# Four image blocks with a selective scan on one Trainium2 core: operands of silu, rows of C and a normalisation move between engines

## Chip, cores, metric

The kernel runs on one core of one Trainium2 chip. The metric is the device time of one execution in microseconds (us). A core has five instruction streams that run beside each other and meet at semaphores: PE (TensorE, matrix products, with its weight loads shown as PEld), DVE (VectorE), ACT (ScalarE), POOL (GpSimd) and SP (SyncE, which here issues DMAs). Each takes its instructions in the order in which they were built.

## What is computed

The input is x, 4 images of 128 channels and 64 x 64 pixels (4096 columns), all in float32. Four layers follow, each adding to x what it makes of the group-normalised x (32 groups): attention over the 4096 pixels, a 5 x 5 convolution whose weights are built from tables, a selective scan, and a 3 x 3 convolution. The change lies mostly in the third:

```python
t = einsum('oc,bchw->bohw', Wx, x) + bx          # 128 channels; halves F and R
# one half, u of 64 channels; R runs over the flipped sequence
xc = silu(sum(conv_w[:, k] * up[:, k:k + L] for k in range(4)) + conv_b)
delta = softplus(xc.T @ Wd + bd);  Bm = xc.T @ WB;  Cm = xc.T @ WC
h = scan over the sequence of  h = exp(delta * A) * h + (delta * xc) * Bm   # 64 states a channel
y = sum over states of h * Cm  +  D * xc
```

## The kernel before

**Stages.** For each image b: attention (`attention_start`, `attention`), the 5 x 5 convolution (`conv_pairs`), then the preparation of the scan (`scan_prep`, `scan_operands`), and at last the scan itself (`scan_core`), 256 ticks an image. Afterwards `scan_end` and the 3 x 3 convolution (`conv`) finish an image. The scan of image b runs beside attention, convolution and preparation of image b + 1: `images` is a generator of all that work, and `program` pulls steps from it between the half-ticks of `scan_core`, by a credit of 2.8 a tick (1.5 for the last image) against the cost that each step yields. So the order on each engine is fixed when the program is built, and buffers and semaphores do the rest.

**One tick of the scan** covers 32 channels x 4 states on 1024 columns: `drive` multiplies on POOL (db, L1027), `decay` takes exp on ACT (da, L1020), `recur` scans on DVE (L1037), the product with C is on DVE (L1040) or on POOL (`weigh`, L1058) by `to_pool`, and `collect` sums on PE into y (L1072), every second tick.

**Preparation.** `scan_operands` cuts the 4096 columns into 8 blocks of 512 (i) and writes out an order by hand: a table of slots, five to a block, with each step at a slot. In image 0 nothing runs beside the first of it. For block i at slot t = 5 i:

- t, t + 1 `taps`: 4 taps x 2 halves = 8 products on PE (L832) into a bank "s", each half on its own 64 columns of the array; for i = 0 an edge term (L838)
- t + 4 `halves`: on ACT, half of the biased sum to xc (L846), and its tanh to th (L851): for image 0 a buffer in SBUF, for the others the bank itself
- t + 5 `silu`: on DVE, xc = (th + 1) * xc (L855)
- t + 8, t + 9, t + 12: the three products on PE with the block-diagonal weights `bdiag` (L864): 0 for delta, 1 for B, 2 for C. B and C share bank "a"
- t + 10 `softplus` (L877, L878), t + 12 `exp` (L904, L909) on ACT; t + 13 `digits` on DVE (L883, L884)
- t + 11 and t + 13 `row`: ACT copies a row block of B (m = 1) or C (m = 2) from PSUM to a buffer "w" (L869, four buffers), and SP writes it to DRAM

After a group of blocks come the logarithms on ACT (`logs`, L913), then `join` and `drives` on POOL (L889, L894).

**Next image.** Beside that, `start(b + 1)` loads the next x, and `attention_start` takes its statistics on DVE (L378), computes scale rs and offset nb on POOL (`group_norm`, L363, L364), normalises x in place in four pieces of 1024 columns on ACT (`piece`, L369 in `normalise`), and makes v: `keys` on PE (L396) and `take` on ACT (L401), for b > 0 in turns in one bank "s".

Of the kernel before, what the change touches and what calls it, by code (L numbers as in the profile page):

```python
# [24 lines left out]
F32 = mybir.dt.float32  # L25
I32 = mybir.dt.int32
AF = mybir.ActivationFunctionType
ALU = mybir.AluOpType
# [4 lines left out]
P = 128  # L33
# [3 lines left out]
MM = 512  # L37
HALF = P // 2
# [7 lines left out]
PRODUCT, HOP, SLOT, PACE, ENDPACE, AHEAD = 0.86, 1.7, 0.7, 2.8, 1.5, 4  # L46


BQ, BK, BX, BP, CONVB, BD, DSKIP, MAINB, CONVW, ALOG = 0, 1, 2, 3, 4, 5, 6, 7, 8, 12
# [3 lines left out]
def conv_preact_kernel(  # L53
# [16 lines left out]
    nc = tc.nc  # L70
# [12 lines left out]
    scale = float(C) ** -0.5  # L83
# [3 lines left out]
    const = ctx.enter_context(tc.tile_pool(name="const", bufs=1))  # L87
# [3 lines left out]
    pools, ready = {}, set()  # L91

    def bank(tag, name):
        return pools.get(tag, ps).tile([P, MM], F32, tag=tag, name=name)
# [20 lines left out]
    ident = const.tile([P, P], F32, name="ident")  # L115
    make_identity(nc, ident)
    ones = const.tile([P, P], F32, name="ones")
# [9 lines left out]
    def col(i):  # L127
        return vec[:, i : i + 1]


    ssm_sb = early.tile([P, 3, HALF], F32, name="ssm_sb")
    nc.scalar.dma_start(ssm_sb, ssm)
    bdiag = const.tile([P, 3, C], F32, name="bdiag")
    nc.gpsimd.memset(bdiag, 0.0)
    for d in range(2):
        r = slice(d * HALF, (d + 1) * HALF)
        nc.gpsimd.tensor_copy(bdiag[r, :, r], ssm_sb[r, :, :])


    NK, NQ = P // SG, NST // NI  # L140
# [10 lines left out]
    skip = const.tile([P, P], F32, name="skip")  # L151
# [25 lines left out]
    wtap = const.tile([P, KC, C], F32, name="wtap")  # L177
    edge = const.tile([P, KC - 1], F32, name="edge")
    cbias = small.tile([P, 1], F32, tag="cbias", bufs=1, name="cbias")
    hbias = const.tile([P, 1], F32, name="hbias")  # L180

    def scan_constants():

        for k in range(KC):
            ptap = bank("z", f"ptap{k}")[:, :C]
            nc.tensor.matmul(
                ptap, col(CONVW + k).to_broadcast([P, P]), ident, start=True, stop=True
            )
            yield HOP
            nc.vector.tensor_tensor(wtap[:, k, :], wm[:, 3, :], ptap, ALU.mult)  # L190
        for t in range(KC - 1):

            nc.vector.tensor_reduce(
                edge[:, t : t + 1], vec[:, CONVW : CONVW + KC - 1 - t], AX.X, ALU.add
            )
        nc.vector.tensor_tensor(cbias, edge[:, 0:1], col(CONVW + KC - 1), ALU.add)
        nc.vector.scalar_tensor_tensor(cbias, cbias, col(BX), col(CONVB), ALU.mult, ALU.add)
        nc.vector.tensor_scalar(edge, edge, col(BX), -1.0, ALU.mult, ALU.mult)
        nc.vector.tensor_scalar(hbias, cbias, 0.5, None, ALU.mult)
        yield HOP  # L200
        mine = early.tile([P, NI], F32, name="mine")
        nc.vector.tensor_reduce(
            mine, ident.rearrange("p (s i) -> p i s", i=NI), AX.X, ALU.add
        )
        rates = every.rearrange("p k q i -> p (k q) i")
        mine = mine.unsqueeze(1).to_broadcast([P, NK * NQ, NI])
        nc.vector.tensor_tensor(rates, rates, mine, ALU.mult)
        nc.vector.tensor_reduce(a_neg, rates, AX.X, ALU.add)
        yield HOP
        nc.scalar.activation(a_neg, a_neg, AF.Exp)  # L210
        nc.vector.tensor_reduce(
            sel, ident.rearrange("p (s i) -> p s i", i=NI), AX.X, ALU.add
        )
        nc.vector.tensor_scalar(skip, ident, col(DSKIP), None, ALU.mult)
        yield HOP
        nc.vector.tensor_scalar(a_neg, a_neg, -1.0, None, ALU.mult)
        yield HOP
# [66 lines left out]
    def large(n, name):  # L284
        return pools["big"].tile([P, ASIZE], F32, tag=f"A{n % 2}", name=name)
# [6 lines left out]
    def stats_tile(name):  # L292
        return small.tile([P, NM, 6], F32, tag=f"gn_st{name[0]}", name=f"st_{name}")
# [74 lines left out]
    def normalise(dst, src, gn):  # L368
        nc.scalar.activation(dst, src, AF.Identity, scale=gn[0], bias=gn[1])  # L369
# [4 lines left out]
    def attention_start(b, xn):  # L374

        st = stats_tile(f"a{b}")
        for i in range(NM):
            nc.vector.bn_stats(st[:, i, :], xn[:, bass.ts(i, MM)])  # L378
            yield 0.0
        gn = yield from group_norm(st, f"a{b}")  # L380
        while b > 0 and (b - 1, "taps") not in ready:
            yield 0.0
        v = pools["big"].tile([P, VSIZE], F32, tag="V", name=f"v_{b}")
        v = v[:, : NJT * C].rearrange("p (j c) -> p j c", c=C)
        pvs = {}

        def piece(i):
            cut = bass.ts(i, L // 4)
            normalise(xn[:, cut], xn[:, cut], gn)

        def keys(i):

            tag = "s" if b > 0 else "saz"[i % 3]
            pvs[i] = bank(tag, f"pv_{b}_{i}").rearrange("p (t c) -> p t c", c=C)
            for t in range(TPM):
                nc.tensor.matmul(  # L396
                    pvs[i][:, t, :], xn[:, bass.ts(i * TPM + t, P)], wv, start=True, stop=True
                )

        def take(i):  # L400
            nc.scalar.copy(v[:, i * TPM : (i + 1) * TPM, :], pvs.pop(i))  # L401

        piece(0)
        yield SLOT
        for i in range(NM):
            if i % 2 == 0 and i // 2 + 1 < 4:
                piece(i // 2 + 1)
            keys(i)
            yield SLOT
            if b > 0:  # L410
                take(i)
                yield 0.0
            elif i > 0:
                take(i - 1)
        if b == 0:
            take(NM - 1)
        return xn, v
# [394 lines left out]
    def scan_operands(b, xn, mats4, piece):  # L812
# [5 lines left out]
        xc = large(b, f"xc_{b}")[:, :L]  # L818
        delta = pools["big"].tile([P, L], F32, tag="xt", name=f"delta_{b}")
        pts, ths, pzs, pbs, us = {}, {}, {}, {}, {}  # L820

        def taps(i, *ks):
            if ks[0] == 0:
                pts[i] = bank("s", f"pt_{b}_{i}")
            pt = pts[i]
            t = i * MM
            for k in ks:
                lo = L + 2 * pad - 1 - k - t - (MM - 1)
                views = (xn[:, t + k : t + k + MM], xn[:, lo : lo + MM][:, ::-1])
                for d, view in enumerate(views):  # L830
                    r = slice(d * HALF, (d + 1) * HALF)
                    nc.tensor.matmul(  # L832
                        pt[r, :], wtap[:, k, r], view,
                        start=k == 0, stop=k == KC - 1,
                        tile_position=(0, d * HALF), skip_group_check=True,
                    )
                    if i == 0 and k == 0:
                        nc.tensor.matmul(  # L838
                            pt[r, : pad], ident[:, r], edge, start=False, stop=False,
                            tile_position=(0, d * HALF), skip_group_check=True,  # L840
                        )

        def halves(i):

            pt = pts.pop(i)
            nc.scalar.activation(xc[:, bass.ts(i, MM)], pt, AF.Identity, scale=0.5, bias=hbias)  # L846

            ths[i] = pt if b > 0 else pools["bg"].tile(
                [P, MM], F32, tag="w", bufs=4, name=f"th_{b}_{i}"
            )  # L850
            nc.scalar.activation(ths[i], pt, AF.Tanh, scale=0.5, bias=hbias)  # L851

        def silu(i):
            cut = bass.ts(i, MM)
            nc.vector.scalar_tensor_tensor(  # L855
                xc[:, cut], ths.pop(i), 1.0, xc[:, cut], ALU.add, ALU.mult
            )
            if i % 2:
                c = i // 2
                nc.sync.dma_start(xcd[c], xc[:, bass.ts(c, CH)])  # L860
# [5 lines left out]

        def row(i, m):
            bs = pools["bg"].tile([P, MM], F32, tag="w", bufs=4, name=f"bs{m}_{b}_{i}")
            nc.scalar.copy(bs, pbs.pop((i, m)))  # L869
            c, h = divmod(i, CH // MM)  # L870
            nc.sync.dma_start(bc[m - 1][c][:, bass.ts(h, MM)], bs)

# [271 lines left out]
    def program(safe):  # L1144
# [113 lines left out]
        with ExitStack() as es, tc.manual_schedule():  # L1258
# [18 lines left out]
            work = images()  # L1277
# [26 lines left out]
            def result():  # L1304

                while (B - 1, "staged") not in ready:
                    next(work)
                return ends[B - 1][2]

            credit = 0.0  # L1310
# [91 lines left out]
```

## Time and profile before

| what | value |
|---|---|
| time, median of 3 runs | 4535.0 us (4529.53 to 4537.47) |
| profiled execution: its time, its span | 4540.09 us, 4538.3 us |
| granted TensorE clock, mean | 0.939 |
| PE busy | 4022.5 us (89%) |
| DVE busy | 3649.1 us (80%) |
| POOL busy | 3636.2 us (80%) |
| ACT busy | 2400.1 us (53%) |
| bias and half, L846 ACT | 32 x 688 ns |
| tanh, L851 ACT | 24 x 660 ns to PSUM, 8 x 689 ns to SBUF |
| row copies, L869 ACT | 64 x 595 ns |
| normalisation of x, L369 ACT | 16 x 1245 ns |
| db, L1027 POOL | 1024 x 2366 ns |

Durations are those of single instructions; on ACT one starts up to 0.12 us before the one ahead of it ends, so that from start to start 128 x 512 takes 0.5 to 0.58 us. PE's ends are modelled: of its instructions the distance between starts is the safer number. An fp32 product stands as two records (passes). The page gives shares of the whole span; the views of the trace (windows, timelines, waits) give the same for any stretch. Where a wait has several causes, the view names the one that came last.

### The profile page before, as it was taken

What the parts mean: (1) busy time and instruction counts of PE and PEld (TensorE: products, weight loads), DVE (VectorE), ACT (ScalarE), POOL (GpSimd) and SP (SyncE); (2) the same over time, 40 slices, a digit from 0 to 9 for tenths busy, and PEclk for the clock granted to TensorE, in tenths of its full rate; (3) what the DMA queues carried; (4) which work ended last, traced back from release to release, by engine and by line L of the source; (5) the groups of instructions that cost most, each with busy time, mean ns of one, the idle gap of its engine ahead of it and who ended that gap; (6) DMA issues with size and microseconds to landing.
All of it is one profiled execution on the core that took longest, in us unless ns stands there. A gap on an engine that the chain in (4) does not pass through costs nothing. (4 is left out here: it accounts for less than half of the span.)

```text
span 4538.3 us, 43660 instructions
## 1 busy us (share of the span) xinstructions
PE 4022.5 (89%) x13568; PEld 1492.3 (33%) x13568; DVE 3649.1 (80%) x3619; ACT 2400.1 (53%) x4420; POOL 3636.2 (80%) x1730
## 2 busy tenths in 40 slices
PE   8999998999999979999999879999999658576767
PEld 4444433333333323333333223333333112121212
DVE  4722106999998978999989879999999699999993
ACT  3333217666665466666654566666654654544441
POOL 3433207999998969999989889999999799999992
PEclk9999999999999989999999989999999878687878
DMA  1000006445544555544545555545445566656561
GB/s 62 6 1 1 5 29 239 175 170 174 175 174 155 181 202 201 175 174 169 179 154 181 185 207 180 169 170 175 175 159 178 211 235 204 231 188 230 186 232 47
DMA packets 210579, 719.48 MB, mean 159 GB/s; under 512 B 24864, under 2 KB 25760, under 8 KB 210208
## 3 DMA queue, kind: packets, MB, share of 16 engines
q1 hardware_dynamic: 208736, 715.87, 44.8%
q8 instruction: 109, 1.79, 0.2%
q14 instruction: 134, 1.10, 0.1%
q10 hardware_dynamic: 1600, 0.73, 0.1%
HBM read 649.07 MB, written 67.44 MB: 158 GB/s over the span
## 5 line engine op out<-in xcount | busy, mean ns | idle before, releaser
L1027 POOL TENSOR_TENSOR db<-dx,br 128x1024 f32<-128x1024 f32 x1024 | 2399.7, 2366 | 234.0 <-DMA dx<-dxd 59.7
L1020 ACT ACTIVATE da<-de,a_neg 128x512 f32<-128x512 f32 (+1 forms) x1795 | 1342.2, 751 | 745.4 <-DVE da L1037 451.2
L464 PE MATMUL sc<-r,x 128*128 128x512 f32 x2048 | 1082.4, 611 | 18.2 <-ACT r L433 12.4
L476 PE MATMUL acc<-pt,v 128*128 128x512 f32 x2048 | 1046.6, 593 | 1.6
L1058 POOL TENSOR_TENSOR hc<-hc,cr 128x1024 f32<-128x1024 f32 x406 | 959.7, 2364 | 14.3 <-ACT last L1053 11.7
L470 ACT ACTIVATE pt<-sc 128x512 f32<-128x512 f32 x1024 | 604.3, 590 | 563.9 <-PE sc L464 555.2
L1072 PE MATMUL y<-hc,sel 128*32 128x512 f32 x4096 | 656.9, 651 | 271.5 <-POOL hc L1058 267.0
L1040 DVE TENSOR_TENSOR hc<-da,cr 128x512 f32<-128x512 f32 (+1 forms) x1067 | 828.4, 776 | 68.9 <-issue 1.8
L1037 DVE TENSOR_TENSOR_SCAN da<-da,last,db 128x512 f32<-128x512 f32 (+1 forms) x464 | 728.2, 1569 | 27.3 <-POOL db L1027 21.7
L1037 DVE TENSOR_TENSOR_SCAN da<-da,da,db 128x512 f32<-128x512 f32 x449 | 577.9, 1287 | 13.6 <-ACT da L1020 12.7
L464 PEld LDWEIGHTS sc<-r,x 128*128 128x128 f32 x2048 | 359.1, 190 | 605.0 <-issue 374.3
L476 PEld LDWEIGHTS acc<-pt,v 128*128 128x128 f32 x2048 | 387.5, 190 | 497.2 <-issue 477.9
L1037 DVE TENSOR_TENSOR_SCAN hc<-da,hc,db 128x512 f32<-128x512 f32 x322 | 413.1, 1283 | 61.2 <-ACT da L1020 30.4
L1037 DVE TENSOR_TENSOR_SCAN hc<-da,last,db 128x512 f32<-128x512 f32 (+1 forms) x304 | 455.9, 1500 | 6.6 <-ACT da L1020 2.4
L518 POOL TENSOR_TENSOR sidep<-sidep,pt 128x512 f32<-128x512 f32 x120 | 170.4, 1420 | 280.0 <-ACT pt L470 277.9
L1072 PEld LDWEIGHTS y<-hc,sel 128*32 128x32 f32 x4096 | 94.7, 111 | 728.5 <-POOL hc L1058 359.5
L643 PE MATMUL pcm<-xpm,cw 128*128 128x512 f32 x576 | 290.5, 652 | 30.5 <-ACT xpm L369 30.5
L760 PE MATMUL pe<-df,cw 128*128 128x512 f32 x640 | 289.5, 598 | 0.0
L518 DVE TENSOR_TENSOR sided<-sided,pt 128x512 f32<-128x512 f32 x120 | 97.2, 810 | 231.0 <-ACT pt L470 229.7
L1037 DVE TENSOR_TENSOR_SCAN da<-da,db 128x512 f32<-128x512 f32 (+1 forms) x154 | 231.2, 1501 | 32.5 <-POOL db L1027 16.4
L498 PE MATMUL zp<-pt,ones 128*32 128x512 f32 x1536 | 204.8, 595 | 5.0 <-DVE xs L562 5.0
L1053 ACT COPY last<-da 128x1 f32<-128x1 f32 x469 | 73.0, 156 | 246.9 <-DVE hc L1040 245.1
(196 smaller groups left out, 2719.5 us busy)
## 6 DMA issues: line engine op xcount, KB each, us to landing
br<-bm SPq DMA_DIRECT2D x512, 512.0 KB, 5.2
cr<-cm SPq DMA_DIRECT2D x512, 512.0 KB, 3.9
de<-dd SPq DMA_DIRECT2D x64, 512.0 KB, 4.6
dx<-dxd SPq DMA_DIRECT2D x64, 512.0 KB, 6.5
x<-in_x_dram SPq DMA_DIRECT2D x16, 512.0 KB, 5.1
xs<-in_x_dram SPq DMA_DIRECT2D x16, 512.0 KB, 5.6
xsd<-xs SPq DMA_DIRECT2D x16, 512.0 KB, 5.1
xcd<-xc SPq DMA_DIRECT2D x16, 512.0 KB, 2.8
```

What stands on the lines that cost most here:

```text
L464: nc.tensor.matmul(sc, xn[:, bass.ts(j, P)], rq[blk], start=True, stop=True)
L470: nc.scalar.activation(pt, sc, AF.Exp)
L476: nc.tensor.matmul(acc[blk], v[:, j, :], ring[:, u % NRING, :], start=j == 0, stop=j == NJT - 1)
L518: eng.tensor_tensor(s, s, ring[:, u % NRING, :], ALU.add)
L643: nc.tensor.matmul(acc.rearrange("p (r w) -> p r w", w=W), weights[:, t, :], xp[:, y : y + RPM, dx : dx + W], start=t == 0, stop=t == k * ...
L760: nc.tensor.matmul(flat(acc), cw[:, w * K5 + dx, :], view(r, dx), start=k == 1, stop=k == total and (n == 0 or not lean),)
L1020: nc.scalar.activation(da, rep["de", b, c, d, g][:, bass.ts(h, size)], AF.Exp, scale=a_neg[:, at(i)])
L1027: nc.gpsimd.tensor_tensor(dbs[i], rep["dx", b, c, d, g], rows["b", b, c, d, q], ALU.mult)
L1037: nc.vector.tensor_tensor_scan(h, da, db[:, cut], before, ALU.mult, ALU.add)
L1040: nc.vector.tensor_tensor(hc[:, cut], h, rows["c", b, c, d, q][:, cut], ALU.mult)
L1058: nc.gpsimd.tensor_tensor(hcs[i], hcs[i], rows["c", b, c, d, q], ALU.mult)
L1072: nc.tensor.matmul(y[r : r + SG, :], sel, hcs[i - KG + 1 + gg][:, bass.ts(h, MM)], start=q == 0, stop=False, tile_position=(0, r), skip_gr ...
```

## The change

1. The weights in `bdiag` are multiplied by 0.5, 0.25 and 0.5 (delta, B, C) and the skip weights by 0.5, which takes up silu's half. Six small POOL instructions stand for two copies. (xc now holds twice silu: delta, C and skip take a half for it, and B a quarter, for itself and for the xc in delta * xc.)
2. silu's bias, until now `hbias` on ACT, becomes a product: a row `brow` of 128 biases is made once by a small product and a copy, and after the first tap of each half a product of one contraction row adds it into the bank. `halves` keeps one ACT instruction of two, tanh to SBUF in every image; silu reads the bank in place of xc.
3. For images 1 to 3, the rows of C leave PSUM on DVE in place of ACT.
4. For images 1 to 3, x is normalised in place on POOL in place of ACT. The order in which SP issues its DMAs is the same as before.

```diff
-        nc.gpsimd.tensor_copy(bdiag[r, :, r], ssm_sb[r, :, :])
+        for m, factor in enumerate((0.5, 0.25, 0.5)):
+            nc.gpsimd.tensor_scalar(bdiag[r, m, r], ssm_sb[r, m, :], factor, None, ALU.mult)
...
-    hbias = const.tile([P, 1], F32, name="hbias")
+    brow = const.tile([1, P], F32, name="brow")
...
-        nc.vector.tensor_scalar(hbias, cbias, 0.5, None, ALU.mult)
+        yield HOP
+        pr = bank("z", "pbrow")
+        nc.tensor.matmul(pr[0:1, :P], cbias, ident, start=True, stop=True)
+        yield HOP
+        nc.vector.tensor_copy(brow, pr[0:1, :P])
...
-        nc.vector.tensor_scalar(skip, ident, col(DSKIP), None, ALU.mult)
+        nc.vector.tensor_scalar(skip, ident, col(DSKIP), 0.5, ALU.mult, ALU.mult)
...
         def piece(i):
+
             cut = bass.ts(i, L // 4)
-            normalise(xn[:, cut], xn[:, cut], gn)
+            if b > 0:
+                nc.gpsimd.tensor_scalar(xn[:, cut], xn[:, cut], *gn, ALU.mult, ALU.add)
+            else:
+                normalise(xn[:, cut], xn[:, cut], gn)
...
                         start=k == 0, stop=k == KC - 1,
                         tile_position=(0, d * HALF), skip_group_check=True,
                     )
+                    if k == 0:
+                        nc.tensor.matmul(
+                            pt[r, :], brow[:, r], ones[0:1, 0:1].to_broadcast([1, MM]),
+                            start=False, stop=False,
+                            tile_position=(0, d * HALF), skip_group_check=True,
+                        )
...
-            pt = pts.pop(i)
-            nc.scalar.activation(xc[:, bass.ts(i, MM)], pt, AF.Identity, scale=0.5, bias=hbias)
-
-            ths[i] = pt if b > 0 else pools["bg"].tile(
-                [P, MM], F32, tag="w", bufs=4, name=f"th_{b}_{i}"
-            )
-            nc.scalar.activation(ths[i], pt, AF.Tanh, scale=0.5, bias=hbias)
+            ths[i] = pools["bg"].tile([P, MM], F32, tag="w", bufs=4, name=f"th_{b}_{i}")
+            nc.scalar.activation(ths[i], pts[i], AF.Tanh, scale=0.5)
...
-                xc[:, cut], ths.pop(i), 1.0, xc[:, cut], ALU.add, ALU.mult
+                xc[:, cut], ths.pop(i), 1.0, pts.pop(i), ALU.add, ALU.mult
...
-            nc.scalar.copy(bs, pbs.pop((i, m)))
+            (nc.scalar.copy if m == 1 or b == 0 else nc.vector.tensor_copy)(bs, pbs.pop((i, m)))
...
-                    next(work)
+                    next(work, None)
```

The last line lets the pull at the end of the scan go on when the generator has run out; no instruction hangs on it.

## Prediction

> **What bounds the kernel now.** I read the page's busy table and slices first. PE, DVE and POOL are all near full for most of the span, so no one engine is the bound everywhere, and the average says little about this change. All its edits but some set-up lie in the *preparation* of an image (`scan_operands` and the start of the next attention). So I cut the span at that stage with the table of windows (columns: window, length, busy us and count of PE, weight load, DVE, ACT, POOL, then PE clock, DMA share, GB/s):
>
> ```profile
> 1400.00:1600.00 200.00, 183.39 (x568) 67.58 (x568) 185.28 (x212) 87.73 (x138) 182.95 (x91) 0.96 0.48 164
> 1600.00:1700.00 100.00, 75.96 (x288) 27.82 (x288) 71.91 (x91) 72.44 (x115) 64.60 (x33) 0.88 0.61 216
> 1700.00:2350.00 650.00, 636.39 (x2401) 234.30 (x2402) 602.58 (x617) 415.40 (x854) 608.82 (x264) 0.99 0.50 177
> ```
>
> The reader is to see the middle row: for 100 us no engine is over 76% busy, while both neighbours hold PE, DVE and POOL over 91%. The same dip stands at 650 to 750, 2560 to 2680 and 3520 to 3625. There a chain sets the pace, and what is put on or off it goes into the total. Elsewhere the change issues almost nothing.
>
> Then I read that chain from the timelines of PE and ACT in image 1 (start, length, engine, line; in brackets the idle time before):
>
> ```profile
> 1620.94 3.66 PE L832 MATMUL pt<-xn,wtap 128*64 128x512 f32 x16
> 1624.53 2.93 PE L864 MATMUL pb<-xc,bdiag 128*128 128x512 f32 x6
> 1627.38 1.06 PE L1072 MATMUL y<-hc,sel 128*32 128x512 f32 x8
> 1629.78 3.66 PE L832 MATMUL pt<-xn,wtap 128*64 128x512 f32 x16 [1.33 <-DVE xc L855]
> ```
>
> ```profile
> 1634.53 0.59 ACT L869 COPY bs<-pb 128x512 f32<-128x512 f32 x1 [3.04 <-PE pb L864]
> 1635.01 0.70 ACT L1020 ACTIVATE da<-de,a_neg 128x512 f32<-128x512 f32 x1
> 1635.63 0.68 ACT L846 ACTIVATE xc<-pt,hbias 128x512 f32<-128x512 f32 x1
> 1636.20 0.66 ACT L851 ACTIVATE pt<-pt,hbias 128x512 f32<-128x512 f32 x1
> ```
>
> One block of 512 columns costs PE 3.66 us of taps and 2.93 us of three products, and every second scan step 1 us of y: 7.6 us with a y. The starts of the taps in image 1 are 1603.4, 1612.7, 1620.9, 1629.8, 1637.6, 1645.2, 1653.1, 1669.4: most periods are 7.6 to 8.8 us. So **PE is nearly full here**, but for 1.33 to 1.35 us in some periods, when it waits for silu (L855), whose tanh stands on ACT behind a row copy (L869), a decay and the half (L846). The waits by total agree:
>
> ```profile
> PEld pt L832 <- DVE xc L855: 52.7, 20, 12.1
> PEld pb L864 <- ACT bs L869: 47.0, 30, 8.0
> ```
>
> **What the skill says.** (1) "TensorEngine Tiling (Array Packing)", Key Properties: tiles of one mode run in parallel, while "Changing tiling mode (not just tile) drains the TensorE". The trace agrees: 16 tap passes in 3.66 us are eight pairs of 0.43, and 8 y passes take 0.99 (1618.03 to the product at 1619.02), i.e. two rounds of 0.43 and some 0.1 for the change of tile shape. A change of the tile's rows is in no row of this trace. (2) "VectorE: DVE Perf Modes", Why PSUM operands drop a tier: fp32 with a PSUM operand runs at 1x. The trace has 686 ns for L884 (PSUM and SBUF in). (3) "GPSIMD Engine Reference", 3.1: about 1.8 cycles per element at best for a one-input loop, 2.6 for two inputs. The trace has COPY 128x512 in 663 ns and TENSOR_TENSOR 128x1024 in 2366 ns.
>
> **The change, part by part.**
>
> *Bias as a product (PE).* Two products are added to each block, one per half: 32 blocks x 2 = 64. They have one contraction row, and the build puts them on a tile of 32 rows by 64 columns, where the taps use 128 by 64; the order by engine is now tap, bias, tap, bias, then six taps. An fp32 product is two passes of 0.43 us here; I take the same for one row. Low bound: the bias of one half runs beside a tap of the other, 2 x 0.43 = 0.86 us a block. Middle: no drain, but a queue that is taken in order pairs only some passes, about 1.75. High: each change of tile drains; then tap, bias, tap, bias stand alone, four products of 0.86 instead of one paired time of 0.86: 3 x 0.86 = 2.57, with four changes of 0.1 **2.95 us a block**. I take the high one: the skill says it, and y and the taps show that tiles of unlike shape don't overlap.
>
> *Half into the weights (ACT).* L846 goes, 32 x 0.58 us (from start to start). Tanh writes SBUF for every image (689 against 660 ns). silu reads pt from PSUM: still one PSUM and one SBUF operand for images 1 to 3, 0.69 us. Its bank "s" is now held until silu in image 0 too: about 0.7 us more, hidden by the 2.93 us of products between two groups of taps.
>
> *Rows of C (ACT to DVE).* 24 copies of 0.5 us leave ACT, 24 come to DVE at 0.48 (SBUF copy L515) to 0.69 (L884), I take 0.65: 16 us, beside a DVE 72% busy here, so nothing on the path. Behind them on DVE stand silu and scans, and SP's write to C waits for them; if DVE were full, the 16 us would be the price. PE's next product into bank "a" waits for this copy as it did for ACT's; product 0 (0.98 us) covers it.
>
> *Normalise (ACT to POOL), images 1 to 3.* 12 pieces of 1.13 us leave ACT; on POOL 2 x 0.663 = 1.33 us at the low end, 2.37 at the high, I take 1.5 (the skill's 1.8 cycles for 1024 elements, an estimate). Four per image, while POOL has 13 us of gaps between 1669 and 1704 (7.06 waiting for dx, 1.84, about 4). Behind each piece stands a db (L1027), and the keys' products wait for it. I cost it at nothing; if POOL were full, 18 to 28 us.
>
> *Rest.* One 128-column product and a 1x128 copy in image 0's attention (0.5 us on a full PE), six small POOL scalings for two copies before 11 us, where POOL waits anyway; SP's order of DMAs is unchanged.
>
> **The sum.** In a period in which PE didn't wait, a block costs +2.95. Where it waited 1.35 for silu, that goes as L869 and L846 leave the chain: +1.6. What is late next is PE itself. The first block of a stage runs partly at half clock and is chained to tanh: about +4.0 - 0.6.
> - Image 0 (nothing beside it at first; period 6.6 = 3.66 + 2.93, PE full): 3.4 + 3 x 2.95; block 4 has a table load on ACT and 1.7 us of slack: 1.25; 3 x 2.95; less 4 pieces (4.5 us) in a stretch where ACT is full (43 of 50 us from 700 to 750): **+18**.
> - Images 1 and 2: 3.4 + 2.95 + 1.6 + 1.6 + 2.95 + 1.6; block 6 nothing (the gap of 16.4 us before block 7 comes from a table load and from group norm on DVE); the last about 4, its clock low after that gap: 18. ACT is full from 1676.5 to 1701 and loses 6.6 us there (three copies, one half, four pieces); the keys' ping-pong in one bank gives back about 4 of it: **+14 each**.
> - Image 3 (no next image): 17 less 1 for ACT: **+16**.
>
> 18 + 14 + 14 + 16 = 62 us. The profiled execution took 4540.1 us (span 4538.3), 5 over the median of three; 4535 + 62 = **4597**.
>
> **Rivals.**
> - *ACT's relief wins (faster).* If the bias overlaps at 0.86 us, image 0 is +6 - 4.5 = +1.5; in images 1 to 3 the four waits of 1.35 go against 0.86 each, which just pays for the other blocks; and the tails of images 1 and 2 keep all of their 6.6: 1.5 - 13 = -12, **4523**. For it: ACT is the fullest engine from 1676 to 1701. Against it: PE's content is 7.6 us of periods of 7.6 to 8.8. It decides from an added time under about 1.2 us a block.
> - *No drain, partial pairs.* 1.75 a block: 25 us over the four images, **4560**.
> - *Hidden.* Bias at 0.86 to 1.2, paid for by ACT's relief: **4535**.
> - *POOL becomes the bound.* Pieces at 2.37 us that push the db's in a POOL that is full from 1710 on: 12 x 2.37 = 28 on top: **4625**.
>
> **Chances.** Forecast 0.45, partial pairs 0.20, POOL 0.10, hidden 0.09, ACT's relief 0.16. About 0.2% (9 us) is what a measurement of this kernel can tell from no change. Slower 0.75, same 0.09, faster 0.16. The range is 4530 to 4625: it leaves out the faster case and little above; the forecast's own range is 4575 to 4615.
>
> **What would show it.** The taps' group of a block from 3.66 to about 6.6 us (4.5: the low bound), with the bias passes alone in their time; the wait of L832 for DVE's xc gone; the stages at 650, 1600, 2560 and 3520 longer by 14 to 18 us, their neighbours unchanged; POOL's pieces at 1.3 to 1.6 us without new waits of PE on them. It is wrong if the bias passes start within 0.01 us of a tap's pass, or if the stages shrink.

## The result, and the profile after

| | before | after |
|---|---|---|
| median of 4 runs each, same chip | 4534.7 us (4529.5 to 4537.5) | 4671.4 us (4670.3 to 4679.2) |
| ratio, 95% interval | | 1.0306 (1.0289 to 1.0324) |
| profiled execution: its time, its span | 4540.1, 4538.3 us | 4679.2, 4677.6 us |
| granted clock, mean over the span, in each of the runs | 0.939 (profile) | 0.931 to 0.936 |

The change costs 137 us. The forecast was 62, and the range ended at 4625, 46 us below the median.

First the place. I cut the span of both kernels at the preparations: from the first tap product of an image to the first exp of the next image's attention. These are the stages of image 0, 1 and 2 after, with the two stretches of scan between them (columns as in the prediction: window, length, busy us and count of PE, weight load, DVE, ACT, POOL, then PE clock, DMA share, GB/s):

```profile
660.00:787.00 127.00, 109.91 (x297) 36.09 (x298) 47.02 (x65) 62.56 (x105) 50.68 (x30) 0.81 0.43 153
787.00:1636.20 849.20, 819.59 (x2993) 300.82 (x2991) 793.33 (x841) 502.54 (x990) 785.55 (x352) 0.99 0.51 175
1636.20:1786.30 150.10, 128.03 (x350) 36.83 (x350) 79.97 (x98) 67.58 (x111) 81.29 (x44) 0.78 0.45 156
1786.30:2633.40 847.10, 822.20 (x2991) 301.47 (x2991) 792.49 (x839) 501.97 (x992) 788.69 (x354) 0.99 0.51 176
2633.40:2787.90 154.50, 123.78 (x358) 35.95 (x358) 85.78 (x99) 68.62 (x113) 87.65 (x47) 0.80 0.43 148
```

Before the change, the same five pieces took 93.7, 849.4, 112.2, 847.9 and 119.3 us. The stretch from the last image's first tap to a point 40 ticks into its scan took 223.7 us before and 259.1 after. So the four preparations grew by 33, 38, 35 and 35 us, about 142 in all, and nothing grew in between: the span grew by 139. The clock column matters as much as the lengths. The stage of image 1 stood before at

```profile
1603.40:1715.50 112.10, 84.99 (x318) 32.63 (x318) 76.09 (x90) 80.33 (x131) 76.67 (x40) 0.87 0.60 209
```

and is now 38 us longer at 0.78, with PE busy 85% of it.

Next the chain. This is PE after the change, in image 0, in a stretch in which full speed is granted (start, length, engine, line, operation; each product is two records):

```profile
697.92 1.07 PE L842 MATMUL pt<-xn,wtap 128*64 128x512 f32 x2
698.92 1.07 PE L848 MATMUL pt<-ones,brow 1*64 1x512 f32 x2
699.92 1.07 PE L842 MATMUL pt<-xn,wtap 128*64 128x512 f32 x2
700.93 1.07 PE L848 MATMUL pt<-ones,brow 1*64 1x512 f32 x2
701.92 2.80 PE L842 MATMUL pt<-xn,wtap 128*64 128x512 f32 x12
704.65 2.93 PE L875 MATMUL pb<-xc,bdiag 128*128 128x512 f32 x6
```

Tap, bias, tap, bias start 1.00 us apart and never meet: 4.0 us for what took one paired 0.9 before. Six taps follow as three pairs in 2.73. The group is 6.73 us from start to start, where it was 3.59 (1620.94 to 1624.53 in the prediction's timeline). That is the forecast's high bound, and a little more.

The same group in image 1:

```profile
1676.90 1.89 PE L842 MATMUL pt<-xn,wtap 128*64 128x512 f32 x2 [2.42 <-DVE xc L866]
1678.73 1.96 PE L848 MATMUL pt<-ones,brow 1*64 1x512 f32 x2
1680.62 1.97 PE L842 MATMUL pt<-xn,wtap 128*64 128x512 f32 x2
1682.52 1.96 PE L848 MATMUL pt<-ones,brow 1*64 1x512 f32 x2
1684.41 4.15 PE L842 MATMUL pt<-xn,wtap 128*64 128x512 f32 x12
1688.50 3.04 PE L875 MATMUL pb<-xc,bdiag 128*128 128x512 f32 x6
1693.59 1.52 PE L842 MATMUL pt<-xn,wtap 128*64 128x512 f32 x2 [2.05 <-DVE xc L866]
```

The lone products start 1.9 us apart in place of 1.00: PE runs at half clock (the view of windows gives 0.50 for this stretch), and stays there through four products that follow each other without a gap. Ahead of this group and of the next PE waits for silu (L866), 2.42 and 2.05 us. DVE in that stretch shows why:

```profile
1678.13 0.69 DVE L895 TENSOR_TENSOR delta<-delta,pb 128x512 f32<-128x512 f32 x1
1689.66 0.69 DVE L880 COPY bs<-pb 128x512 f32<-128x512 f32 x1 [10.85 <-PE pb L875]
1690.27 1.27 DVE L1048 TENSOR_TENSOR_SCAN hc<-da,last,db 128x512 f32<-128x512 f32 x1
1691.58 1.28 DVE L1048 TENSOR_TENSOR_SCAN hc<-da,hc,db 128x512 f32<-128x512 f32 x1
1692.78 0.66 DVE L866 SCALAR_TENSOR_TENSOR xc<-th,pt 128x512 f32<-128x512 f32 x1
```

DVE stands idle for 10.85 us ahead of the copy of a row of C, because product 2, whose result it copies, stands on PE behind the whole longer group of taps. silu, whose tanh ended at 1689.2 on ACT, follows only after the copy and two scan steps. These are groups of instructions over the whole span (busy us, mean ns of one, idle time before and its releaser):

```profile
L842 PE MATMUL pt<-xn,wtap 128*64 128x512 f32 x512 | 212.7, 788 | 67.9 <-DVE xc L866 33.9 <-ACT xn L375 33.6
...
L848 PE MATMUL pt<-ones,brow 1*64 1x512 f32 x128 | 90.1, 791 | 0.0
...
L880 DVE COPY bs<-pb 128x512 f32<-128x512 f32 x24 | 16.5, 689 | 104.7 <-PE pb L875 104.7
...
L397 POOL TENSOR_SCALAR x<-x,rs_a,nb_a 128x1024 f32<-128x1024 f32 x12 | 14.4, 1202 | 0.0
```

Three readings. The bias passes are 90 us of PE, and the taps, unchanged in number, went from 136.8 to 212.7: they lost their partners and, where the clock is halved, speed. DVE was idle 104.7 us ahead of 24 copies. And PE's wait for silu (33.9) is what it was before (35.8), though two instructions had left the chain to it on ACT. These give three suspects: the shape of the bias product, the clock, and the copy on DVE.

### The profile page after: what moved, and what is told of

It reads as the page before. It is cut to its first block, busy times and chain, and to the rows that moved or that the text cites. A ratio compares the mean times of both kernels' runs of the same rounds, so it can differ in the third digit from the quotient of the medians.

```text
span 4677.6 us, 43900 instructions
## 1 busy us (share of the span) xinstructions
PE 4174.8 (89%) x13698; PEld 1510.4 (32%) x13698; DVE 3662.2 (78%) x3643; ACT 2355.5 (50%) x4352; POOL 3642.9 (78%) x1746
## 5 line engine op out<-in xcount | busy, mean ns | idle before, releaser
L1048 DVE TENSOR_TENSOR_SCAN da<-da,last,db 128x512 f32<-128x512 f32 (+1 forms) x464 | 728.2, 1569 | 25.1 <-POOL db L1038 18.9
L842 PE MATMUL pt<-xn,wtap 128*64 128x512 f32 x512 | 212.7, 788 | 67.9 <-DVE xc L866 33.9
```

The costliest lines, as they stand in the source:

```text
L1048: nc.vector.tensor_tensor_scan(h, da, db[:, cut], before, ALU.mult, ALU.add)
```

## The experiments

Theory after the result: (a) the one-row products run alone, +3.1 us a block; (b) something else, in the clock, in DVE's order or in both, makes the rest. Rivals: the bias costs all of it by its mere passes; DVE's copies or POOL's pieces cost most of it; ACT's relief is there and hides under the loss. Medians are of 4 to 20 runs each, beside before at 4530 to 4534 us on the same chip. The input's biases are all zero, so the weights of the bias products hold zeros in every variant; only their geometry differs.

### How the bias is multiplied

**no_bias.** Of the whole change, only the bias product is taken out.

```diff
-                    if k == 0:
-                        nc.tensor.matmul(pt[r, :], brow[:, r], ...)
```

> Leaves out the bias of silu (the product is not issued; all else as in the changed kernel). Theory A: all of the 137 us come from the product of one row, by its serial passes (3.1 us a block, 100 us over 32 blocks at most) and by the lower clock that they bring. Then the time falls to 4510 to 4535, with the four preparations at 85 to 115 us as in the kernel before, and half-clock time in them back near 21, 30 and 41 us. Theory B: a part comes from the moves (copies on VectorE, pieces on GpSimd, the bank held to silu, fewer free buffers for tanh): the time stays at 4555 to 4600.

Measured: 4544.4 us, ratio 1.0025 (1.0016 to 1.0035). 127 of the 137 us need the bias product. But what is left is no gain: the rest of the change costs 12 us, which the forecast had at a gain of at least 13. Neither expectation had this time; it lies between them.

**one_row_paired.** The same one-row products, behind both halves' first taps: two changes of tile a block in place of four.

```diff
                 for d in range(2):
...
-                    if k == 0:
-                        nc.tensor.matmul(pt[r, :], brow[:, r], ...)
...
+                for d in range(2 if k == 0 else 0):
+                    r = slice(d * HALF, (d + 1) * HALF)
+                    nc.tensor.matmul(pt[r, :], brow[:, r], ...)
```

> The two bias products of a block stand together behind both halves' first tap, so that they can run beside each other on their tile of 32 rows; two changes of tile in place of four. Theory A: the group costs 0.86 + 0.2 = 1.06 us a block in place of 3.1, the time falls by at least 32 x 2.1 = 66 us, to 4530 to 4600 (lower if the clock comes back with it). If it is the single row itself that lowers the clock (little of the array works), half-clock time in the preparations stays above that of the kernel before and the time is over 4570. Theory B: a fall of less than 40 us.

Measured: 4593.1 us, 1.0128 (1.0111 to 1.0145). PE in image 0:

```profile
693.62 1.08 PE L842 MATMUL pt<-xn,wtap 128*64 128x512 f32 x4
694.62 1.08 PE L854 MATMUL pt<-ones,brow 1*64 1x512 f32 x4
695.63 2.80 PE L842 MATMUL pt<-xn,wtap 128*64 128x512 f32 x12
```

Two one-row products side by side pair as well as two taps do. The order alone is worth 78 us. A pair beside a change of tile takes 1.00 us from start to start, and 0.87 to 0.91 without one (next run): **about 0.1 us for a change of tile** (0.09 to 0.14).

**full_rows_in_order** and **full_rows_paired.** The same sum by a product of 128 rows, in the taps' own tile: `bdia` is a diagonal of biases. The first keeps the order tap, bias, tap, bias (its edit is shown); the second has tap, tap, bias, bias.

```diff
-        nc.tensor.matmul(pr[0:1, :P], cbias, ident, start=True, stop=True)
+        nc.vector.tensor_scalar(bdia, ident, cbias, None, ALU.mult)
...
-                            pt[r, :], brow[:, r], ones[0:1, 0:1].to_broadcast([1, MM]),
+                            pt[r, :], bdia[:, r], ones[:, 0:1].to_broadcast([P, MM]),
```

> The bias comes from a 128-row product (a diagonal matrix of the biases with ones) in the tile of the taps, in the changed kernel's order tap, bias, tap, bias: no change of tile. Drain as the cause: passes now pair in part, 1.75 us a block, time 4540 to 4590. If order alone makes them serial: 2.6 us a block and 4630 to 4660.

> The 128-row bias in the order tap, tap, bias, bias, all in one tile shape: 0.86 us a block and full pairs. Theory A: 4515 to 4550, the best of the four that keep the bias; if ACT's relief is worth what the rival said, under 4535. Theory B: over 4570.

Measured: 4563.3 us, 1.0072 (1.0055 to 1.0089), and 4565.4, 1.0074 (1.0058 to 1.0091). The two can't be told apart. The second missed its range (4515 to 4550). PE of full_rows_in_order:

```profile
697.36 1.09 PE L840 MATMUL pt<-xn,wtap 128*64 128x512 f32 x4 [0.45 <-DVE xc L864]
698.27 1.04 PE L846 MATMUL pt<-ones,bdia 128*64 128x512 f32 x4
699.14 2.75 PE L840 MATMUL pt<-xn,wtap 128*64 128x512 f32 x12
```

The order tap, bias, tap, bias runs as two full pairs all the same: 0.87 us for the bias. So the order as such costs nothing; the loss needs the other tile shape. The expectation was met by luck: its range stood on passes that pair only in part (the 1.75 us of the prediction's middle estimate), and here all of them pair.

**full_rows_serial.** Is the loss of 4.0 us in place of 0.9 all there is? Here the bias has 128 rows but tiles of 32 columns, two beside each other in a half: as serial as the change, at full rows.

```diff
-                    if k == 0:
+                    for q in range(2 if k == 0 else 0):
+                        s = slice(d * HALF + q * 32, d * HALF + (q + 1) * 32)
-                            pt[r, :], brow[:, r], ones[0:1, 0:1].to_broadcast([1, MM]),
+                            pt[s, :], bdia[:, s], ones[:, 0:1].to_broadcast([P, MM]),
...
-                            tile_position=(0, d * HALF), ...
+                            tile_position=(0, d * HALF + q * 32), ...
```

> A 128-row bias in four tiles of 32 columns, in the changed kernel's order: tap, bias (two tiles beside each other), tap, bias. As many changes of tile and as many passes alone as in the changed kernel, but all 128 rows of the array at work in them. If one row at work lowers the clock: the taps' group still takes about 6.8 us at full clock, but half-clock time in the preparations falls to 20 to 45 us and the time to 4615 to 4645. If it is passes on half of the columns with drains between them: like the changed kernel, 4660 to 4680.

Measured: 4629.4 us, 1.0213 (1.0196 to 1.0230), with the starts of the change itself:

```profile
698.57 1.07 PE L840 MATMUL pt<-xn,wtap 128*64 128x512 f32 x2
699.57 1.05 PE L847 MATMUL pt<-ones,bdia 128*32 128x512 f32 x4
...
702.54 2.80 PE L840 MATMUL pt<-xn,wtap 128*64 128x512 f32 x12
```

So with equal serial time a block (3.97 against 4.00 us), 42 us of the change are missing. The stages of images 0 and 1 of this kernel show where:

```profile
660.50:775.60 115.10, 95.96 (x330) 30.95 (x330) 48.34 (x66) 62.51 (x105) 50.22 (x30) 0.94 0.47 169
1624.90:1755.00 130.10, 106.98 (x382) 32.01 (x382) 79.98 (x98) 67.59 (x112) 81.48 (x44) 0.93 0.51 180
```

The clock is 0.94 and 0.93 where the change has 0.81 and 0.78. (These two profiles are the fastest execution of the one and the slowest of the other; the medians are 42 us apart.) The clock was also higher in every execution: means over the span of 0.943 to 0.945 here, 0.931 to 0.936 there. An estimate of size from the median means, 0.935 of 4671 us and 0.944 of 4629: if PE is always at full or at half speed, it is at half speed for 2 x 0.065 x 4671 = 607 us against 2 x 0.056 x 4629 = 518 us. That is 89 us more, of which half is lost: 44 us, if PE sets the pace all that time. 42 us were measured. The paired runs say the same: one_row_paired (4593 us, median clock 0.939) is 28 us over full_rows_paired (4565 us, 0.943). Its two changes of tile a block make 6 to 9 us of that, and the estimate from the clock makes 20.

**bias_32_rows** and **bias_64_rows.** What is it in the one-row product that goes with the low clock? These keep the order and the 64 columns of the change, and give the row 31 or 63 rows of zeros for company.

```diff
-    brow = const.tile([1, P], F32, name="brow")
+    brow = const.tile([32, P], F32, name="brow")
+    nc.gpsimd.memset(brow, 0.0)
...
-                            pt[r, :], brow[:, r], ones[0:1, 0:1].to_broadcast([1, MM]),
+                            pt[r, :], brow[:, r], ones[0:32, 0:1].to_broadcast([32, MM]),
```

> The changed kernel with the bias product on 32 rows (31 of them zero weights) in place of 1: the same tile of 32 by 64, the same order, the same changes of tile, the same passes; only the number of rows at work differs. If rows at work set the clock (the 128-row serial run had 4629 against 4671): half-clock time in the preparations falls part of the way and the time lies at 4630 to 4665. If it is the tile of 32 rows or the kind of change that lowers it, 4665 to 4680.

> The changed kernel with the bias product on 64 rows (63 of them zero weights), so on a tile of 64 by 64 in the same order: still serial, still four changes of tile that alter its rows. With 1 row the time was 4671, with 32 rows 4660 (half-clock time in the preparations of images 1 and 2 unchanged at 64), with 128 rows in tiles of 32 columns 4629 (19 and 28 us). If the share of the array at work sets the clock: half-clock time falls to 20 to 45 us and the time to 4625 to 4645. If a change of the tile's rows is what brings the low clock, whatever the rows at work: 4650 to 4670.

Measured: 4659.7 us, 1.0281 (1.0264 to 1.0299), and 4657.6, 1.0279 (1.0262 to 1.0296). Means of the clock: 0.936 to 0.938 and 0.936 to 0.939. The stages of images 0 and 1 with 32 rows:

```profile
661.10:780.30 119.20, 100.78 (x298) 33.64 (x298) 47.75 (x65) 62.62 (x105) 50.24 (x30) 0.89 0.46 163
1629.00:1779.00 150.00, 127.90 (x350) 37.01 (x350) 79.96 (x98) 67.67 (x112) 81.33 (x44) 0.79 0.45 156
```

and with 64:

```profile
660.70:779.30 118.60, 100.86 (x298) 33.44 (x298) 48.32 (x66) 62.54 (x105) 50.21 (x30) 0.90 0.46 164
1628.00:1768.50 140.50, 117.59 (x350) 34.61 (x350) 79.94 (x98) 67.66 (x112) 81.31 (x44) 0.86 0.47 167
```

Going from 1 row to 32, at a tile of the same shape, brings back about 10 us; the intervals of the two ratios overlap at their ends, so the time alone doesn't settle it. The profiles point the same way in image 0, where PE comes to the stage in both after an idle 6.92 us. First 32 rows, then the change:

```profile
670.00:680.00 10.00, 8.59 (x24) 2.54 (x23) 0.69 (x1) 0.60 (x1) 0.00 (x0) 0.86 0.00 0
670.00:680.00 10.00, 8.59 (x16) 1.72 (x12) 0.69 (x1) 0.60 (x1) 0.00 (x0) 0.67 0.00 0
```

PE is equally busy, at another clock. In the 10 us after that, the clock is 1.00 with 32 rows and 0.82 with one. change_rows_on_act below, with the same one-row product, repeats the 0.67. In image 1 the clock is 0.79 with 32 rows, 0.86 with 64 and 0.93 with 128, in one execution each: the slowest of its four for 32 rows, the fastest for 64 and for 128. The medians for 32 and 64 rows are 2 us apart, so that step isn't shown to count.

**full_rows_32_columns.** Is it then the share of the array at work? This is full_rows_serial with one tile of 32 columns in each half in place of two, which leaves out the bias of the other 32: 128 rows by 32 columns are a quarter of the array, as 64 rows by 64 columns are.

```diff
-                    for q in range(2 if k == 0 else 0):
+                    for q in range(1 if k == 0 else 0):
```

> The serial run with 128 rows, but only the first 32 of each half's 64 columns get their bias (the bias of the other 64 channels is left out): the bias passes stand alone on 32 columns, a quarter of the array, as in the run with 64 rows by 64 columns, and no change of tile alters its rows. Order, passes in series and changes of tile are those of the changed kernel. If the share of the array at work sets the clock: like the run with 64 rows, 4645 to 4665, half-clock time in the preparations of images 1 and 2 at 35 to 55 us. If changes of the tile's rows bring the low clock: like the 128-row serial run, 4620 to 4638, with 15 to 30 us.

Measured: 4625.7 us, 1.0212 (1.0195 to 1.0229), clock 0.942 to 0.946; stages of images 0 and 1:

```profile
661.80:776.80 115.00, 96.35 (x298) 31.32 (x298) 47.88 (x66) 62.52 (x105) 50.20 (x30) 0.92 0.48 169
1625.20:1758.20 133.00, 110.79 (x350) 32.54 (x350) 80.05 (x98) 67.65 (x111) 81.33 (x44) 0.89 0.51 176
```

It behaves as full_rows_serial does and not as bias_64_rows. So equal shares of the array at work give 32 us of difference: the share is not it, the rows are. Whether by how many rows of the product are at work, or by the change of the tile's rows, these runs don't separate: from 64 to 128 both change together, and most of the loss lies there (28 of 42 us). 1 against 32 rows, where the tile is the same, is for the number. The time of bias_64_rows is for the change of the tile's rows: it fell into the range expected for that.

### What else the change moves

**no_bias_rows_on_act** and **full_rows_rows_on_act.** The copies of C's rows go back to ACT, in no_bias and in full_rows_paired.

```diff
-            (nc.scalar.copy if m == 1 or b == 0 else nc.vector.tensor_copy)(bs, pbs.pop((i, m)))
+            nc.scalar.copy(bs, pbs.pop((i, m)))
```

> Leaves out the bias of silu, and the rows of C leave by ScalarE again. In the run without bias alone, VectorE stands idle at the row copy until PE has product 2, which stands behind the block's taps; scan and silu stand behind it (periods of 10.0 to 11.2 us in blocks 2 to 4 of images 1 to 3, time 4544). If that wait is the loss: periods back to 7.0 to 8.5 us and 4505 to 4530. If the loss is in the pieces on GpSimd or the buffers for tanh: 4538 to 4550.

> The 128-row bias in pairs (4565 with the rows of C on VectorE), and the rows of C leave by ScalarE again. If the row copy is the loss: lower by 20 to 35 us, 4530 to 4545, so that the half and the normalisation just pay for 0.86 us of bias a block. Otherwise 4558 to 4570.

Measured: 4528.2 us, 0.9988 (0.9981 to 0.9995), and 4546.8, 1.0034 (1.0022 to 1.0047). The copies on DVE cost 16 and 19 us. A reason can be read in DVE's timeline of no_bias, image 1:

```profile
1627.44 0.69 DVE L889 TENSOR_TENSOR delta<-delta,pb 128x512 f32<-128x512 f32 x1
1632.65 0.69 DVE L874 COPY bs<-pb 128x512 f32<-128x512 f32 x1 [4.52 <-PE pb L869]
1633.26 1.27 DVE L1042 TENSOR_TENSOR_SCAN hc<-da,last,db 128x512 f32<-128x512 f32 x1
1634.57 1.28 DVE L1042 TENSOR_TENSOR_SCAN hc<-da,hc,db 128x512 f32<-128x512 f32 x1
1635.77 0.66 DVE L860 SCALAR_TENSOR_TENSOR xc<-th,pt 128x512 f32<-128x512 f32 x1
```

DVE stands 4.52 us before the copy, with the scan and silu behind it; in the change the same wait is 10.85.

**change_rows_on_act.** The same edit on the whole change.

> The whole change but its third part: the rows of C leave by ScalarE again. Without the bias VectorE's copy cost 16 us (4544 against 4528), with a 128-row bias 19 (4565 against 4547). In the changed kernel VectorE stands idle for 105 us in all before its 24 copies, as product 2 stands behind longer taps. If the wait grows with the taps it blocks: 4615 to 4648, i.e. 25 to 55 us of the 137. If it costs the same 16 to 19 us whatever the taps: 4650 to 4657. If the taps hide it: 4662 to 4675.

Measured: 4639.1 us, 1.0241 (1.0224 to 1.0258): **32 us**, the double of what the copies cost without the bias. Two terms of the loss are thus not independent. The longer the taps' group ahead of product 2, the longer DVE stands: 30.5 us in no_bias, 40.2 in full_rows_paired, 104.7 in the change. The copies on ACT here wait as long as all copies do in the change, where it was 104.7 us on DVE and 33.6 on ACT:

```profile
L880 ACT COPY bs<-pb 128x512 f32<-128x512 f32 x64 | 38.0, 594 | 135.6 <-PE pb L875 135.6
```

135.6 us of idle time ahead of copies, and yet 32 us less. What differs is what stands behind them: on DVE the scan and silu, on ACT neither. PE's wait for silu falls from 33.9 to 25.1 us only. The clock is higher too (0.936 to 0.940), and by the estimate used above (median 0.9375 against 0.935) about 14 of the 32 us are the clock's. What remains is close to the 16 to 19 us that the copies cost without the one-row bias. Whether the longer waits lower the clock, these runs don't show.

**before_rows_on_dve** and **before_normalise_on_pool.** One part alone on the kernel before: part 3, then part 4.

```diff
-            nc.scalar.copy(bs, pbs.pop((i, m)))
+            (nc.scalar.copy if m == 1 or b == 0 else nc.vector.tensor_copy)(bs, pbs.pop((i, m)))
```

```diff
-            normalise(xn[:, cut], xn[:, cut], gn)
+            if b > 0:
+                nc.gpsimd.tensor_scalar(xn[:, cut], xn[:, cut], *gn, ALU.mult, ALU.add)
+            else:
+                normalise(xn[:, cut], xn[:, cut], gn)
```

> The kernel before with one part of the change: the rows of C of images 1 to 3 leave by VectorE. By my prediction: nothing on the path, 4525 to 4540. If the copy's wait holds up scan and silu: 4550 to 4580, and only in the preparations of images 1 to 3.

> The kernel before with one part of the change: x of images 1 to 3 is normalised by GpSimd, the bias stays on ScalarE. By my prediction 4 us in each of the preparations of images 0 to 2, 4520 to 4530. If GpSimd's pieces push its products: 4535 to 4550.

Measured: 4539.9 us, 1.0014 (1.0007 to 1.0020), and 4530.8, 0.9998 (0.9989 to 1.0007). Part 3 costs 6 us alone, little but clear of noise, and inside the range for "nothing on the path"; part 4 costs nothing that can be measured. The copies of part 3 wait as long here (29.9 us on DVE) as in no_bias (30.5), where they cost 16: so the idle time ahead of a copy isn't its price either. Why the prices differ stays open.

**no_bias_half_alone.** Only the half in the weights and tanh to SBUF: the bias is left out, and copies and normalisation stay on ACT.

> Leaves out the bias of silu; of the change only the half in the weights is left (one ScalarE instruction a block less), rows of C and normalisation stay on ScalarE. With both, 4528. If the half is what was gained: 4525 to 4531. If the normalisation was: 4532 to 4540.

Measured: 4523.9 us, 0.9982 (0.9975 to 0.9989). Eight us is all that 32 instructions fewer on ACT are worth, and tanh's place in the buffers that it now shares with the row copies costs nothing that shows. no_bias_rows_on_act, which has part 4 on top of it, is 4 us slower (4528.2), but the intervals of the two ratios overlap.

## Why the prediction was wrong, and where its mechanism was right

The prediction had the direction, the place and the drain of PE right. Two terms of its sum failed: it left the granted clock as it was but for the first and last blocks (42 us measured), and it put the rows of C at "nothing on the path" (16 us on the ladder, 32 in the change). ACT's relief came out smaller than forecast, too.

The runs can be put in a ladder, each step one edit: before 4532; the half in the weights 4524 (-8); normalisation on POOL 4528 (+4); rows of C on DVE 4544 (+16); the bias, serial at full rows, 4629 (+85); the same with one row 4671 (+42). The steps were measured on several chips, on which the medians of before differ by up to 4 us, so a step of 4 says little. Beside it the forecast's steps:

| step of the forecast | forecast | measured |
|---|---|---|
| bias alone on PE, gross (22.5 + 18 + 18 + 17, ACT's part taken out) | +75 | +85 |
| clock of PE (one row in place of 128, at equal serial time) | none, but for the first and last blocks of a stage | +42 |
| rows of C on DVE | "nothing on the path" | +16 on the ladder (+6 alone on before, +32 as the last step to the change) |
| ACT's relief, with the half, the copies and the pieces | -13 | -8 + 4 |
| sum | +62 | +139 on the ladder, +137 in the direct comparison |

The +85 has the copies' longer wait in it (74.0 us of idle time on DVE ahead of them in full_rows_serial, 30.5 in no_bias). Point by point:

- **Each change of tile drains: right.** The Trainium skill has it in "TensorEngine Tiling (Array Packing)", Key Properties, that a change of tiling mode drains TensorE; the trace agrees, with four products that stand alone at starts 1.00 us apart. The term was mis-sized by little: 3.1 us a block against 2.95. PE's waits for silu, 1.35 us a period in the forecast, were hardly given back (35.8 us before, 33.9 after): silu had got a new obstacle, the copy on DVE.
- **The clock: a step that failed, by 42 us.** I took "half clock" as something that befalls the first block after a gap, and held everything else at 0.86 us a product. The Trainium skill suggests it: "TensorE: Matmul & The Clock Gate", Part 1, has the clock follow PE's busy-ness over windows of about 3.4 us. These traces don't agree with busy-ness alone. In both kernels PE comes to the first product of image 0's stage after an idle 6.92 us; the first line is from before, the others from the change:

```profile
660.00:670.00 10.00, 8.40 (x32) 3.61 (x34) 0.69 (x1) 4.85 (x6) 0.00 (x0) 0.81 0.00 0
660.00:670.00 10.00, 10.00 (x18) 2.49 (x20) 0.00 (x0) 3.30 (x3) 0.00 (x0) 0.50 0.00 0
...
680.00:690.00 10.00, 10.00 (x25) 2.63 (x24) 1.92 (x3) 3.52 (x6) 0.00 (x0) 0.82 0.29 98
```

  PE of the changed kernel has no gap within either stretch, and is granted half speed in all of the first and 0.82 in the second. Before, PE was back at full speed after part of the first, and from 670 to 710 it had 1.00. The profile of before held a hint: its preparations, where PE was busy 76%, had a clock of 0.87 and 0.88, so the range should have left room for a further fall.
- **Rows of C on DVE: the other step that failed, by 16 to 32 us.** I counted 24 x 0.65 us on an engine "72% busy" and got the duration right (0.689). What I left out is the wait that the copy brings with it: on DVE it waits for product 2, which stands behind the next block's taps. The prediction names silu and scans behind the copy, but asks only whether DVE is full. The length of an instruction doesn't give the price of moving it: that also hangs on what it waits for and on what stands behind it in the new queue.
- **ACT's relief: too high.** The chain to silu did lose L869 and L846, and the half alone is worth 8 us. The pieces moved to POOL give nothing (0.9998 alone). In the change PE and its weight loads wait for these pieces four times, 13.2 us in all.
- **POOL: right.** 1.202 us a piece against 1.5 taken and 1.33 as the low end, no idle time on POOL ahead of it, and alone on before no cost that shows in the time. The rival "POOL becomes the bound" (4625) fell, as did "ACT's relief wins": even with no bias at all and with the copies on DVE the kernel is 12 us slower than before. "Hidden" would have needed the bias at 0.86 us a block; at 0.87 the kernel is still 31 us over before (full_rows_in_order), so its estimate was wrong as well; with the copies on ACT it is 13 (full_rows_rows_on_act).
- **The signs asked for:** the group of taps at about 6.6 us (6.73) and the bias passes alone in their time came true. The stages grew by 33 to 38 us and not by 14 to 18; the waits of L832 for silu are not gone: that of PE's weight load, shown in the prediction, went from 52.7 to 16.7 us, that of PE itself from 35.8 to 33.9. The first need not be a relief: the idle time of the weight loads ahead of the taps for which the view names no releaser rose from 58.0 to 146.7 us.

What stays open: why few-row products lower the clock. Fewer rows go with a lower mean clock (0.934, 0.936, 0.937, 0.944 for 1, 32, 64 and 128 rows, about; 32 and 64 can't be told apart), and yet more than half of each preparation of the change runs at full clock (the clock record of the trace has 47.6 of 127.0 us at half clock in image 0, and 64.6 of 150.1 in image 1), with the same products in it. Rows at work and change of the tile's rows aren't separated, and that the clock watches the rows at work is argued, not shown; nor were weights other than zero tried in these products. A way to add the bias without a product and with one ACT instruction a block wasn't tried.

No variant that keeps the bias beats the kernel before by more than can be told: before_normalise_on_pool is at 0.9998.

## What to carry to other kernels

Add a small product to a PE stage only in the tile shape of its neighbours: a bias by a 128-row diagonal cost 19 us here, the same bias by one row 127. Before moving a PSUM copy to another engine, look up what the copy waits for and what stands behind it in the new queue; the busy share of that engine didn't tell here. And put a clock term in the sum for each stage in which the granted clock already lies below 1.

## What the runs showed of the hardware that I had not expected

- A lone fp32 product of 512 columns takes 1.00 us from start to start when its neighbours have another tile shape, a pair in the same shape 0.87 to 0.91 us: about 0.1 us for a change.
- In one tile shape, products for the two halves of the columns pair even when they are issued first both for one half and then both for the other (tap, bias, tap, bias: 0.87 us for the added two).
- PE without a gap was granted half speed for 10 us (660 to 670 in the changed kernel, after 6.92 us of idling; before, the clock of the same stretch was 0.81). Serial products of 1 to 64 rows between those of 128 went with a mean clock of about 0.936, those of 128 rows, on 32 columns too, with about 0.944.
- POOL takes 1.202 us for x * scale + offset, both by pointer, on 128 x 1024 fp32 in place: 1.17 ns an element, about 1.8 times a 128 x 512 copy (0.663 us).
